# A graph layer and an attention layer on one core: two sets of transposes on TensorE, or through DRAM with block transposes on VectorE

## The chip, the cores and the metric

The kernel runs on one core of a Trainium2 chip. The metric is the device time of one execution in microseconds (us), lower is better. Three executions of the kernel before took 2546.09, 2548.84 and 2551.68 us; the median is 2548.84. The profile is that of another execution, with a span of 2546.3 us from the first to the last instruction. The engines are TensorE (PE in the profile, with its weight loads as PEld), VectorE (DVE), ScalarE (ACT), GpSimd (POOL) and SyncE (SP), which issues all DMAs of this kernel from one queue, in order.

## The reference

The input x is (16 batches, 1024 nodes, 256 channels), all in float32. Layer 0 is a graph convolution with two batch norms, a residual and a layer norm. Layer 1 weights the adjacency matrix by a function of the means of the rows, derives queries from it, and attends with 4 heads of 64 channels:

```python
x = _layernorm(x + _L0_gnn_ref(...))            # x1 below: the normalised rows
# layer 1, per batch; fea is x1 transposed
c_adj = mean over channels of x1
A = abs(abs(sigmoid(c_adj[m] - c_adj[n]) - 0.5) - 0.5) * 2.0
g = relu(einsum('cn,nm->cm', fea, adj * A) * para)   # queries, as g transposed
k, v = x1 @ kv_w, split
out = softmax(q k^T * scale) v                       # 4 heads
x = _layernorm(x1 + out)
```

Two transpositions follow from this. Keys and values are products of x1 with channels on the partitions (x1T), while the layer norm and the graph product need x1 with nodes on the partitions. And the sums of values (ot, channels on the partitions, nodes along the row) have to be turned back into rows of nodes before they are divided by the softmax denominators, added to x1 and normalised.

## The kernel before, in words

Layer 0 takes the first 815 us or so and is not touched. Its result y lies in DRAM (yT), with channels first. Layer 1 is `fast()`. It works through the 16 batches in a pipeline of three depths: while batch b attends, the graph product, keys and values of batch b+1 and the normalised rows of batch b+2 are made.

The order of the work is written out by hand. A batch has 16 *steps*; a step is 16 matmuls of scores (L739), two exponentials on ScalarE (L751), 16 matmuls of values (L770, into the PSUM tiles o) and two additions of the exponentials on VectorE into acc (L760, or L757 for the first step of a head pair). Half `hf` of the nodes and pair `pair` of the heads change every four steps: (half 0, pair 0), (0, 1), (1, 0), (1, 1). All other work is cut into pieces, which `put(w, t, f, ...)` places into *slots*, eight to a batch (slot 8w + t). Two slots and then four steps are issued in turn, so that a batch consists of four such groups. I call them quarters 0 to 3: quarter 0 is slots 0 and 1 and the steps of (half 0, pair 0), and so on. `arrange` orders the pieces of a slot: `dens` and `bn2_q` first, the pieces of TensorE (keys, values, graph) with the short ones (`short`) spread among them, the rest by `rank` (the list `order`), and the gates (`wg_a`, `wg_b`, ScalarE and VectorE) spread over the whole. The first addition of a quarter, `sums(g)`, is placed after the last short piece of its two slots. Every engine executes its share in the order of issue.

The pieces that matter here:

- `load` (slots 0 to 3, tiles j = 0 to 3 of 256 rows): four DMAs of 32x32 blocks of y from DRAM into the buffer yt (L432; the pool has two buffers) and one of x (L436).
- `bn2_q` (slot j+1): two operations on GpSimd over yt (L599).
- `rows` (slot j+2): VectorE's 32x32 block transpose from yt into x1 (L603) and the residual (L604). With the blocks fetched in the right places, this makes a full transposition. So y already takes this way.
- `ln1_a`, `ln1_b` (slots j+2, j+3): layer norm of x1; `means` (slot 6) and `crow` (slot 7): the row of means, transposed on TensorE (L659) and spread over all partitions by way of DRAM.
- `x1_t` (slot j+4): four transposes of 128x128 on TensorE into PSUM (px, L638), and a copy into x1T on ScalarE (L639; on VectorE for batch 0).
- `keys` and `values` (slots 0 to 2), `wg_a`/`wg_b` (slots 0 to 3), `graph` (slots 3 to 7) of batch b+1.
- At the end of a pair's four steps, `attend` joins both PSUM tiles of values into ot (a copy on ScalarE, L781, and an addition on VectorE, L782).
- `dens` (slots 4 and, for half 1, 8, that is slot 0 of the next batch): matmuls of acc with ones (pd, L791). They need all additions of the half just ended. `recips` (one slot later): transposes (pr) and reciprocals into RD (L804).
- `finish_a` (slots 5, 6 and 9, 10): four transposes of ot on TensorE (pf, L813), VectorE's multiplication by RD out of PSUM (L817), GpSimd's addition of x1 (L822). `finish_s`: statistics (L547, L548) and the factors on GpSimd. `finish_b`: normalisation on ScalarE (L838) and the store of the result (L841).

Before the first batch attends, the pieces of batch 1's rows are issued in eight slots of their own, beside the graph product of batch 0 (`opening`), without steps between them.

Of the kernel before, what the change touches and what calls it, by code (L numbers as in the profile page):

```python
# [9 lines left out]
F32 = mybir.dt.float32  # L10
# [6 lines left out]
P = 128  # L17
# [5 lines left out]
def gnn_norm_attention_kernel(  # L23
# [28 lines left out]
    dram = ctx.enter_context(tc.tile_pool(name="dram", bufs=1, space=DRAM))  # L52
    ctx.enter_context(tc.manual_schedule())

    ident = const.tile([P, P], F32, name="ident")
# [25 lines left out]
    Q = 32  # L81
    NQ = P // Q
    y_blk = [yT_all[b].rearrange("i (d e) (q n) -> q e (i d) n", e=Q, q=NQ) for b in range(B)]
    st2_dram = dram.tile([2, C], F32, name="st2_d")

    c_dram = [dram.tile([NT, P], F32, name=f"crow_d{b}") for b in range(B)]
# [33 lines left out]
    with ExitStack() as l0:  # L120
# [32 lines left out]
        with ExitStack() as ph1:  # L153
# [9 lines left out]
            for i in range(0, NT, 2):  # L163
                t = hp.tile([P, 2, N], F32, tag="h", name=f"A{i}")
# [22 lines left out]
            KB = FB // P  # L187
# [6 lines left out]
            for h in range(NH):  # L194
                rows = range(h * KB, (h + 1) * KB)
                for i in rows:
                    blk = A[i][:, ts(i, P)]
# [8 lines left out]
                for j in range(NT):  # L206
                    p = ps.tile([P, FB], F32, tag="ah"[j % 2], name="pat")
# [25 lines left out]
            for c in range(HT):  # L233
                p = ps.tile([P, FB], F32, tag="a", name="pw1")
# [3 lines left out]
            for c in range(CT):  # L238
                p = ps.tile([P, FB], F32, tag="a", name="pw2")
# [142 lines left out]
            for f in range(HT):  # L382
                for h in range(NH):
# [3 lines left out]
                    p = hidden(B - 1, h, f)  # L387
# [7 lines left out]
        ldp = right("ldp", LDP)  # L395
# [43 lines left out]
        with ExitStack() as ph2:  # L439
# [74 lines left out]
            for k, pair in enumerate(pairs):  # L514
# [23 lines left out]
    NP = HEADS // 2  # L538
# [17 lines left out]
    def fast():  # L556
      with ExitStack() as fx:
# [9 lines left out]
        otp = pool("otp", 3)  # L567
# [52 lines left out]
        def ln1_b(b, j):  # L620
            mv, rs = mvs.pop((b, j))
            for a in range(2):
# [8 lines left out]
                    accum_out=css[b][:, 2 * j + a : 2 * j + a + 1],  # L631
                )

        def x1_t(b, j):
            p = ps_t.tile([P, CT, 2 * P], F32, tag="t", name="px")
            for a in range(2):
                for c in range(CT):
                    nc.tensor.transpose(p[:, c, ts(a, P)], x1s[b, j][:, a, ts(c, P)], ident)  # L638
            (nc.vector.tensor_copy if b == 0 else nc.scalar.copy)(x1Ts[b][:, :, ts(j, 2 * P)], p)  # L639

        def means(b):
            nc.vector.tensor_scalar_mul(css[b], css[b], 1.0 / C)
# [84 lines left out]
        def step(g):  # L727
            b, s = divmod(g, NS)
            hf, pair, cp = s // (NP * NT // 2), s // (NT // 2) % NP, s % (NT // 2)
            return b, hf, pair, cp  # L730
# [22 lines left out]
        def sums(g):  # L753
# [4 lines left out]
            else:  # L758
                for a in range(2):
                    nc.vector.tensor_add(ACC[b, hf, pair], ACC[b, hf, pair], E[g, a])  # L760

        def attend(g):
            b, hf, pair, cp = step(g)
            if cp == 0:
                O[b, hf, pair] = [ps_t.tile([P, FB], F32, tag="t", name=f"o{g}_{r}") for r in range(2)]
            for a in range(2):
                cb = 2 * cp + a
                for r in range(2):
                    for h in range(2):
                        nc.tensor.matmul(  # L770
                            O[b, hf, pair][r][h * HD : (h + 1) * HD, :],
                            vs[b][r * HD : (r + 1) * HD, cb, pair * P + h * HD : pair * P + (h + 1) * HD],
                            E[g, a][r * HD : (r + 1) * HD, h, :],
                            start=(cb == 0),
                            stop=(cb == NT - 1),
                        )
                E.pop((g, a))
            if cp == NT // 2 - 1:
                t = otp.tile([P, FB], F32, tag=f"ot{pair}", bufs=2 - pair, name=f"ot{g}")
                o = O.pop((b, hf, pair))  # L780
                nc.scalar.copy(t, o[0])  # L781
                nc.vector.tensor_add(t, o[1], t)  # L782
                OT[b, hf, pair] = t

        def dens(b, hf):
            p = ps_t.tile([P, FB], F32, tag="t", name="pd")
# [10 lines left out]
        KB = FB // P  # L797

        def recips(b, hf):
# [5 lines left out]
                RD[:, i : i + KB, :], p.rearrange("p k (h r) -> p k h r", r=32)[:, :, :, 0]  # L805
            )

        def finish_a(b, j):
            hf, k = divmod(2 * j, KB)
            p = ps_t.tile([P, 2, C], F32, tag="t", name="pf")  # L810
            for a in range(2):
                for pair in range(NP):
                    nc.tensor.transpose(p[:, a, ts(pair, P)], OT[b, hf, pair][:, ts(k + a, P)], ident)  # L813
            pool_r = (rp, "r") if b < B - 1 else (x1p, "x1")
            r = pool_r[0].tile([P, 2, C], F32, tag=pool_r[1], name=f"r_{b}_{j}")
            rd = RD[:, b * NT + 2 * j : b * NT + 2 * j + 2, :].rearrange("p a h -> p (a h)")
            nc.vector.tensor_mul(  # L817
                r.rearrange("p a (h d) -> p (a h) d", h=HEADS),
                p.rearrange("p a (h d) -> p (a h) d", h=HEADS),
                rd.unsqueeze(2).to_broadcast([P, 2 * HEADS, HD]),  # L820
            )
            (nc.gpsimd if b < B - 1 else nc.vector).tensor_add(r, r, x1s.pop((b, j)))  # L822
            R[b, j] = r
# [52 lines left out]
        def put(w, t, f, *a):  # L876
            at.setdefault(w * NC + t, []).append((f, a))
# [4 lines left out]
        for b in range(B):  # L882

            for hf in range(NH):
                t = (hf + 1) * (NC // NH)
                put(b, t, dens, b, hf)
                put(b, t + 1, recips, b, hf)
                for k in range(KB // 2):
                    put(b, t + 1 + k, finish_a, b, hf * (KB // 2) + k)
                    put(b, t + 1 + k, finish_s, b, hf * (KB // 2) + k)  # L890
                    late = NC - t - 2 - k if b == B - 1 and hf == 0 else 0
                    put(b, t + 2 + k + late, finish_b, b, hf * (KB // 2) + k)
            if b == 0:
                continue

            put(b - 2, 2, begin, b)
            for j in range(NT // 2):
                put(b - 2, j, load, b, j)
                put(b - 2, j + 1, bn2_q, b, j)
                put(b - 2, j + 2, rows, b, j)  # L900
                put(b - 2, j + 2, ln1_a, b, j)
                put(b - 2, j + 3, ln1_b, b, j)
                put(b - 2, j + 4, x1_t, b, j)
            put(b - 2, NC - 2, means, b)
            put(b - 2, NC - 1, crow, b)

            i = 0
            for t, n in enumerate(WG):
                for i in range(i, i + n):
                    put(b - 1, t, wg_a, b, i)  # L910
                    put(b - 1, t, wg_b, b, i)
                i += 1
            kv = [(keys, (b, c, h)) for c in range(CT) for h in range(NH)]
            kv += [(values, (b, j)) for j in range(0, NT, 2)]
            for t, n in enumerate(KV):
                for _ in range(n):
                    f, a = kv.pop(0)
# [9 lines left out]
        nsteps = B * NS  # L927


        order = (dens, recips, finish_a, finish_b, x1_t, rows, ln1_a, ln1_b, finish_s, means, load, crow)  # L930
        rank = {f: k for k, f in enumerate(order)}
        short = (dens, recips, finish_a, x1_t, crow)
        long = (keys, values, graph)

        def spread(few, many):
# [143 lines left out]
        )  # L1079

    flag = fast()


# [153 lines left out]
```

## Time and profile before

| engine | busy us of 2546.3 | share |
|---|---|---|
| TensorE (PE) | 2487.9 | 98% |
| VectorE (DVE) | 1730.6 | 68% |
| ScalarE (ACT) | 1078.3 | 42% |
| GpSimd (POOL) | 865.3 | 34% |

| group of instructions | count | busy us | mean ns |
|---|---|---|---|
| TensorE transposes of x1, px L638 | 256 | 40.7 | 282 |
| TensorE transposes of ot, pf L813 | 256 | 40.2 | 280 |
| VectorE block transposes of y, L603 | 60 | 42.1 | 702 |
| VectorE additions into acc, L760 | 384 | 515.8 | 1343 |
| ScalarE copies into x1T, L639 | 60 | 35.1 | 586 |
| DMAs of 64 KB of y blocks, L432 | 240 | | |

Matmuls are pipelined, so that the busy time of a group on TensorE counts overlapping instructions; the distance between their starts is what one occupies. In the timeline, a row joins equal instructions that follow each other ("x4"), and a bracket at its end says how long the engine was idle before it and what ended the idle time. The DMA share of the 16 DMA engines is about 0.16 in the attention part, at 38 GB/s. A batch takes 105.8 us there, from one pd to the same pd of the next batch.

### The profile page before, as it was taken

How to read it: one execution, taken by the hardware profiler on the slowest of the kernel's cores; microseconds unless marked ns; L12 is line 12 of the kernel's file. 1: busy time of each engine (PE TensorE's matmuls, PEld its weight loads, DVE VectorE, ACT ScalarE, POOL GpSimd, SP SyncE). 2: the span in 40 equal slices, each digit the busy share in tenths (PEclk: the TensorE clock that was granted, in tenths of full speed). 3: DMA queues.
4: the chain of work that ended last, by engine and by line, in shares of the span. 5: the costliest groups of instructions: out<-in, count | busy, mean ns of one | idle time of the engine just before them, and what ended most of it. 6: DMA issues, size and time to landing. Idle time of an engine off the chain costs nothing. (4 is left out here: it accounts for less than half of the span.)

```text
span 2546.3 us, 33280 instructions
## 1 busy us (share of the span) xinstructions
PE 2487.9 (98%) x12813; PEld 1067.4 (42%) x12813; DVE 1730.6 (68%) x2594; ACT 1078.3 (42%) x1385; POOL 865.3 (34%) x766
## 2 busy tenths in 40 slices
PE   8999999998998999999999999999999999999997
PEld 4444444443443444344443444434444344443432
DVE  5545554556776776786877768777687776877556
ACT  2000000004453455465554655546556465564644
POOL 2222322222555323342433324333243332432132
PEclk9999999999999999999999999999999999999998
DMA  3122222230885201111111111111111111110000
GB/s 132 66 89 93 99 74 91 83 141 21 301 297 173 59 18 46 43 29 34 26 46 46 26 34 26 46 46 26 34 26 46 47 25 34 27 48 27 9 13 23
DMA packets 233349, 163.79 MB, mean 64 GB/s; under 512 B 136680, under 2 KB 221280, under 8 KB 226016
## 3 DMA queue, kind: packets, MB, share of 16 engines
q1 hardware_dynamic: 233184, 161.60, 21.1%
q8 instruction: 103, 1.69, 0.3%
q14 instruction: 62, 0.51, 0.1%
HBM read 98.58 MB, written 62.98 MB: 63 GB/s over the span
## 5 line engine op out<-in xcount | busy, mean ns | idle before, releaser
L751 ACT ACTIVATE e<-s 128x1024 f32<-128x1024 f32 x512 | 495.8, 1020 | 361.9 <-PE s L739 311.5
L760 DVE TENSOR_TENSOR acc<-acc,e 128x1024 f32<-128x1024 f32 x384 | 515.8, 1343 | 72.7 <-ACT e L751 42.6
L739 PE MATMUL s<-qT,kT 64*64 64x512 f32 x4096 | 492.4, 596 | 13.9 <-ACT e L751 13.2
L770 PE MATMUL o<-e,v 64*64 64x512 f32 x4096 | 486.4, 590 | 0.0
L713 PE MATMUL pg<-wg,x 128*128 128x512 f32 x960 | 434.5, 594 | 0.0
L822 POOL TENSOR_TENSOR r<-r,x 128x512 f32<-128x512 f32 x60 | 105.7, 1761 | 572.3 <-ACT wg L671 261.1
L739 PEld LDWEIGHTS s<-qT,kT 64*64 64x64 f32 x4096 | 147.2, 133 | 309.6 <-issue 250.9
L770 PEld LDWEIGHTS o<-e,v 64*64 64x64 f32 x4096 | 157.0, 133 | 284.1 <-issue 271.4
L599 POOL TENSOR_TENSOR yt<-yt,stq 128x512 f32<-128x512 f32 x120 | 192.4, 1603 | 193.2 <-DMA yt<-yT 188.3
L713 PEld LDWEIGHTS pg<-wg,x 128*128 128x128 f32 x960 | 172.3, 190 | 175.9 <-issue 166.1
L98 ACT COPY u<-pa 128x512 f32<-128x512 f32 x15 | 8.8, 585 | 475.3 <-PE pa L303 475.3
L680 DVE SCALAR_TENSOR_TENSOR wg<-wg,adj_sb 128x1024 f32<-128x1024 f32 x128 | 156.3, 1239 | 67.3 <-ACT wg L676 65.0
L303 PE MATMUL pa<-AhT,x 128*128 128x512 f32 x360 | 161.8, 592 | 0.0
L688 PE MATMUL pk<-x1T,kvw 128*128 128x512 f32 x256 | 118.4, 606 | 1.3 <-DVE x1T L639 1.3
L639 ACT COPY x1T<-px 128x512 f32<-128x512 f32 x60 | 35.1, 586 | 191.4 <-PE px L638 190.6
L699 PE MATMUL pv<-kvw,x1T 128*128 128x256 f32 x512 | 115.7, 379 | 0.0
L721 DVE TENSOR_TENSOR qT<-pg,para_sb 128x512 f32<-128x512 f32 x64 | 44.2, 690 | 101.7 <-PE pg L713 100.8
L334 PE MATMUL ph<-agg,SW 128*128 128x512 f32 x240 | 112.8, 592 | 0.0
L66 POOL TENSOR_SCALAR rs_a<-mv_a 128x2 f32<-128x2 f32 x64 | 20.5, 320 | 258.3 <-DVE mv_a L548 258.3
L303 PE MATMUL pa<-T,sx 128*128 128x512 f32 x240 | 107.9, 592 | 0.0
L303 PEld LDWEIGHTS pa<-AhT,x 128*128 128x128 f32 x360 | 68.4, 190 | 86.1 <-issue 86.1
L782 DVE TENSOR_TENSOR ot<-o,ot 128x512 f32<-128x512 f32 x64 | 44.0, 688 | 87.8 <-ACT ot L781 87.8
(193 smaller groups left out, 3332.4 us busy)
## 6 DMA issues: line engine op xcount, KB each, us to landing
h<-hT SPq DMA_DIRECT2D x28, 1024.0 KB, 4.4
hL<-h SPq DMA_DIRECT2D x28, 1024.0 KB, 9.2
x<-in_x_dram SPq DMA_DIRECT2D x16, 1024.0 KB, 7.3
yT<-y SPq DMA_DIRECT2D x64, 256.0 KB, 2.5
out_dram<-r SPq DMA_DIRECT2D x64, 256.0 KB, 2.1
xr<-in_x_dram SPq DMA_DIRECT2D x62, 256.0 KB, 2.9
yt<-yT SPq DMA_DIRECT2D x240, 64.0 KB, 2.9
crow<-crow_d SPq DMA_DIRECT2D x15, 512.0 KB, 4.0
```

Of the source, the lines that this page charges most:

```text
L303: nc.tensor.matmul(p, xs[n][:, k, :], bs[n][:, k, :], start=(k == 0), stop=(k == KN - 1))
L334: nc.tensor.matmul(p, ws[n][:, ts(f, P)], bs[n], start=True, stop=True)
L599: nc.gpsimd.tensor_tensor(y, y, sc, op)
L680: nc.vector.scalar_tensor_tensor(t, t, 1.0, adj_sb[:, i, :], op0=OP.add, op1=OP.mult)
L688: nc.tensor.matmul(p, kvw[:, k, ts(c, P)], x1Ts[b][:, k, ts(h, FB)], start=(k == 0), stop=(k == CT - 1))
L699: nc.tensor.matmul(p[:, ts(a, C)], x1Ts[b][:, k, ts(j + a, P)], kvw[:, k, C:], start=(k == 0), stop=(k == CT - 1),)
L713: nc.tensor.matmul(pg[b], x1s[b, k // 2][:, k % 2, ts(c, P)], wgs[b, k][:, ts(h, FB)], start=(k == 0), stop=(k == NT - 1))
L739: nc.tensor.matmul(t[r * HD : (r + 1) * HD, h, :], kTs[b, pair][h * HD : (h + 1) * HD, ts(2 * cb + r, HD)], qTs[b, pair, hf][h * HD : (h + ...
L751: nc.scalar.activation(E[g, a], S.pop((g, a)), AF.Exp)
L760: nc.vector.tensor_add(ACC[b, hf, pair], ACC[b, hf, pair], E[g, a])
L770: nc.tensor.matmul(O[b, hf, pair][r][h * HD : (h + 1) * HD, :], vs[b][r * HD : (r + 1) * HD, cb, pair * P + h * HD : pair * P + (h + 1) * HD],
L822: (nc.gpsimd if b < B - 1 else nc.vector).tensor_add(r, r, x1s.pop((b, j)))
```

## The change

Both transpositions leave TensorE. The normalised rows x1 of batches 1 to 15 are written to DRAM (`put_x1`, two DMAs per tile), read back by 32x32 blocks (`get_x1`, four DMAs, into a buffer of the pool that y uses) and turned by a block transpose on VectorE straight into x1T (`x1_v`). ScalarE's copy goes. The sums of values ot are written to DRAM at the end of a pair (one DMA in `attend`), read back by blocks (`fetch_o`, four DMAs, one buffer) and turned on VectorE inside `finish_a`, whose multiplication then reads SBUF. Only the last half of the last batch (`by_pe`) and the rows of batch 0 keep TensorE. Keys are made half by half instead of channel block by channel block. In the list of short pieces, `x1_t` is gone and nothing takes its place.

```diff
+        def put_x1(b, j):
+            for c in range(CT):
+                nc.sync.dma_start(
+                    x1_dram[b, j][c].rearrange("(a p) f -> p a f", p=P), x1s[b, j][:, :, ts(c, P)]
+                )
+
+        def get_x1(b, j):
+            t = XB[b, j] = ldp.tile([P, CT * 2 * P], F32, tag="yt", name=f"xb{b}_{j}")
+            blk = x1_dram[b, j].rearrange("c (m n) (q f) -> q n (c m) f", n=Q, q=NQ)
+            for q in range(NQ):
+                nc.sync.dma_start(
+                    t[q * Q : (q + 1) * Q].rearrange("p (m f) -> p m f", f=Q), blk[q]
+                )
+
+        def x1_v(b, j):
+            nc.vector.transpose(x1Ts[b][:, :, ts(j, 2 * P)], XB.pop((b, j)).rearrange("p (c n) -> p c n", c=CT))
...
-            (nc.vector.tensor_copy if b == 0 else nc.scalar.copy)(x1Ts[b][:, :, ts(j, 2 * P)], p)
+            nc.vector.tensor_copy(x1Ts[b][:, :, ts(j, 2 * P)], p)
...
+        def by_pe(b, hf):
+            return b == B - 1 and hf == NH - 1
...
-                t = otp.tile([P, FB], F32, tag=f"ot{pair}", bufs=2 - pair, name=f"ot{g}")
+                t = otp.tile([P, FB], F32, tag=f"ot{pair}", bufs=1, name=f"ot{g}")
...
-                OT[b, hf, pair] = t
+                if by_pe(b, hf):
+                    OT[b, hf, pair] = t
+                else:
+                    nc.sync.dma_start(
+                        o_dram[b, hf][:, ts(pair, P), :].rearrange("i p n -> p i n"),
+                        t.rearrange("p (i n) -> p i n", n=P),
+                    )
...
+        def fetch_o(b, j):
+            hf, k = divmod(2 * j, KB)
+            if by_pe(b, hf):
+                return
+            t = OB[b, j] = otp.tile([P, 2, C], F32, tag="ob", bufs=1, name=f"ob{b}_{j}")
+            blk = o_dram[b, hf].rearrange("i (d e) (q n) -> q e (i d) n", e=Q, q=NQ)
+            for q in range(NQ):
+                nc.sync.dma_start(
+                    t[q * Q : (q + 1) * Q].rearrange("p a (d n) -> p (a d) n", n=Q),
+                    blk[q][:, ts(k // 2, 2 * C // Q), :],
+                )
...
+                p = r
+                nc.vector.transpose(
+                    r.rearrange("p a c -> p (a c)"), OB.pop((b, j)).rearrange("p a c -> p (a c)")
+                )
...
+                    put(b, t + k, fetch_o, b, hf * (KB // 2) + k)
                     put(b, t + 1 + k, finish_a, b, hf * (KB // 2) + k)
...
-                put(b - 2, j + 4, x1_t, b, j)
+                put(b - 2, j + 3, put_x1, b, j)
+                put(b - 2, j + 4, get_x1, b, j)
+                put(b - 2, j + 5, x1_v, b, j)
...
-            kv = [(keys, (b, c, h)) for c in range(CT) for h in range(NH)]
+            kv = [(keys, (b, c, h)) for h in range(NH) for c in range(CT)]
...
-        order = (dens, recips, finish_a, finish_b, x1_t, rows, ln1_a, ln1_b, finish_s, means, load, crow)
+        order = (dens, recips, finish_a, fetch_o, finish_b, x1_v, rows, ln1_a, ln1_b, put_x1, get_x1, finish_s, means, load, crow)
         rank = {f: k for k, f in enumerate(order)}
-        short = (dens, recips, finish_a, x1_t, crow)
+        short = (dens, recips, finish_a, crow)
```

More of the change, by code (lines that the diff above doesn't have):

```diff
@@ L83, in gnn_norm_attention_kernel @@
     y_blk = [yT_all[b].rearrange("i (d e) (q n) -> q e (i d) n", e=Q, q=NQ) for b in range(B)]
+    o_dram = {(b, h): dram.tile([NT // NH, C, P], F32, name=f"o{b}_{h}") for b in range(B) for h in range(NH)}
+    x1_dram = {
+        (b, j): dram.tile([CT, 2 * P, P], F32, name=f"x1_{b}_{j}") for b in range(1, B) for j in range(NT // 2)
+    }
     st2_dram = dram.tile([2, C], F32, name="st2_d")
@@ L632, in ln1_b @@
                 )
+        XB = {}
+        def put_x1(b, j):
[12 more added lines that the diff above has]
+            nc.vector.transpose(x1Ts[b][:, :, ts(j, 2 * P)], XB.pop((b, j)).rearrange("p (c n) -> p c n", c=CT))
         def x1_t(b, j):
@@ L806, in recips @@
             )
+        OB = {}
+        def fetch_o(b, j):
[9 more added lines that the diff above has]
+                )
         def finish_a(b, j):
             hf, k = divmod(2 * j, KB)
[L810 to L813, printed above, removed]
             pool_r = (rp, "r") if b < B - 1 else (x1p, "x1")
             r = pool_r[0].tile([P, 2, C], F32, tag=pool_r[1], name=f"r_{b}_{j}")
+            if by_pe(b, hf):
+                p = ps_t.tile([P, 2, C], F32, tag="t", name="pf")
+                for a in range(2):
+                    for pair in range(NP):
+                        nc.tensor.transpose(p[:, a, ts(pair, P)], OT[b, hf, pair][:, ts(k + a, P)], ident)
+            else:
+                p = r
+                nc.vector.transpose(
+                    r.rearrange("p a c -> p (a c)"), OB.pop((b, j)).rearrange("p a c -> p (a c)")
+                )
             rd = RD[:, b * NT + 2 * j : b * NT + 2 * j + 2, :].rearrange("p a h -> p (a h)")
```

## The prediction

> **What bounds the kernel now.** I read the page's busy shares first, then TensorE's waits in the attention part, the timeline of one batch (number 6 of 0 to 15, 1511 to 1618 us) engine by engine, and the DMA issues.
>
> ```profile
> PE 2487.9 (98%) x12813; PEld 1067.4 (42%) x12813; DVE 1730.6 (68%) x2594; ACT 1078.3 (42%) x1385; POOL 865.3 (34%) x766
> ...
> PE s L739 <- ACT e L751: 5.6, 14, 0.6
> PE pd L791 <- DVE acc L760: 0.4, 2, 0.2
> ...
> 1559.87 1.90 PE L770 MATMUL o<-e,v 64*64 64x512 f32 x16
> 1561.70 1.05 PE L791 MATMUL pd<-acc,ones 128*32 128x512 f32 x4
> 1562.96 1.05 PE L791 MATMUL pd<-acc,ones 128*32 128x512 f32 x4 [0.21 <-DVE acc L760]
> 1563.95 0.66 PE L638 MATMUL px<-ident,x 128*128 128x128 f32 x4
> ```
>
> TensorE hardly waits: from batch to batch the same instruction returns every 105.8 us. But one of its two short waits matters: at the start of quarter 2 the sums matrix (pd) waits for VectorE's last addition. VectorE, 68% busy on average, is on the path there:
>
> ```profile
> 1521.18 1.23 DVE L680 SCALAR_TENSOR_TENSOR wg<-wg,adj_sb 128x1024 f32<-128x1024 f32 x1 [1.12 <-ACT wg L676]
> 1522.33 0.68 DVE L817 TENSOR_TENSOR r<-pf,RD 128x512 f32<-128x512 f32 x1
> 1522.93 1.22 DVE L757 TENSOR_TENSOR acc<-e,e 128x1024 f32<-128x1024 f32 x1
> 1525.32 0.43 DVE L547 BATCH_NORM_STATS2 st_z<-r 128x6 f32<-128x256 f32 x1 [1.17 <-POOL r L822]
> ...
> 1540.83 0.70 DVE L603 STREAM_TRANSPOSE x<-yt 128x512 f32<-128x512 f32 x1
> ...
> 1553.53 9.38 DVE L760 TENSOR_TENSOR acc<-acc,e 128x1024 f32<-128x1024 f32 x6
> 1562.83 0.69 DVE L782 TENSOR_TENSOR ot<-o,ot 128x512 f32<-128x512 f32 x1
> ```
>
> From 1525.3 to 1562.9 no idle time stands in front of any VectorE line: in quarters 0 and 1 it is full, and its end (1562.9) releases TensorE (1562.96). In quarters 2 and 3 it has some 18 us of idle in 54.
>
> ```profile
> 1497.08 2.02 SPq L432 DMA_DIRECT2D yt<-yT  x4
> ...
> yT<-y SPq DMA_DIRECT2D x64, 256.0 KB, 2.5
> yt<-yT SPq DMA_DIRECT2D x240, 64.0 KB, 2.9
> ```
>
> SP issues in order, about 0.5 us for each DMA of 32-float pieces. The loads for quarter 0 leave at 1497, in quarter 3 before it.
>
> **What the Trainium skill says.** "TensorE: Matmul & The Clock Gate", Part 4, gives a TensorE transpose some 275 ns in a kernel and says a copy must follow. The trace shows that duration (273 ns), but four start within 0.44 us: 0.109 us is what one occupies. "VectorE: DVE Perf Modes", The three transpose paths: VectorE transposes 32x32 blocks only; here 0.70 us for 128x512. "DMA: Bandwidth & Descriptors", Two DMAs through the same engine are not ordered: a read of what another DMA wrote must wait, on the issuing engine, for the first one's semaphore. The trace agrees: crow's read is issued 1.2 us after its write (1495.46, 1496.68). "SBUF — State Buffer", Who interferes with whom: a VectorE instruction with two SBUF inputs and a GpSimd one that reads SBUF shut each other out. The trace shows it: an addition L760 takes 1.23 us, beside L599 on POOL 1.88.
>
> **The change, part by part.** Against the profile's span, 2546.3 us; the three runs have a median of 2548.8, so I add the difference to that.
>
> (a) TensorE, quarters 2 and 3. Each batch from 0 to 13 loses here four x1 tiles (px) and two tiles of finish_a (pf): 24 transposes x 0.109 = 2.6 us. No wait of its own hides this: -2.6 x 14 = -36.6. The copies on ACT that go (0.59 us each) were beside other work: 0.
>
> (b) Quarters 0 and 1. Two pf tiles go (0.87 us), but TensorE only arrives earlier at the pd that waits for VectorE: worth 0. VectorE gains two transposes there; instructions overlap by 0.08, so 0.62 each. The x1 transpose that moves into quarter 0 falls in the idle time after 1512.9: 0. Multiplying from SBUF instead of PSUM is about the same (0.69), if POOL leaves the port. Against this, finish_s now comes after one gate pair more in the written order, so the 1.17 us wait for POOL is filled. In sum -1.17 + 0.62 + 0.62, and 0.5 for POOL's L599 now beside it (see c): 0.6 us later at pd. Batches 1 to 13: +7.8. Bounds: 0 (all filled) to 2.0 (two transposes, a blocked multiplication 0.66, nothing filled).
>
> (c) SP. Every batch gets 44 DMAs more: 8 puts and 16 gets of x1, 4 writes and 16 reads of o; at 0.48 us that is 21 us of a queue mostly idle. The order is what matters. The write of o waits for L782 (1512.95), lands 2.5 later; the four reads then go out 1515.5 to 1517.5 and land by about 1519.3 (L432's loads: 3.6 us from first issue to last landing); finish_a's transpose is due at 1522.4: 3 us of slack. The next batch's load, issued at 1497 before, stands behind them: landed at 1521.2. POOL's L599 for it (3.2 us) now runs ahead of finish_a's addition L822, which ends about 1526.7 rather than 1525.27; VectorE asks for it at about 1526.6 to 1527.2. So hidden, barely. In quarter 2 the reads land at 1571, due 1575; x1's come at 1574, due 1578. In quarter 3 the get for tile 2 lands at 1494.5 in the frame of the batch before, VectorE stands about 3 us for it, and its next work (L721) waited 5.1 us for TensorE anyway: 0.
>
> (d) crow's transpose moves to the front of slot 7, before its 14 matmuls of graph, since x1_t no longer shares them. It needs the means, which VectorE reaches after a transpose of o and one of x1: due at 1490.15, ready at 1490.2 to 1490.6. +0.3 x 14 = +4.2; bounds 0 and 1.0.
>
> (e) Batch 14 (its quarters have no x1 work, VectorE has slack): four pf tiles, -1.7.
>
> (f) The opening. There is no attention between the slots there. In before VectorE transposes at 866.67 and queries start at 872.87:
>
> ```profile
> 866.67 0.70 DVE L603 STREAM_TRANSPOSE x<-yt 128x512 f32<-128x512 f32 x1
> ...
> 872.87 0.69 DVE L721 TENSOR_TENSOR qT<-pg,para_sb 128x512 f32<-128x512 f32 x1 [0.87 <-PE pg L1006]
> ```
>
> Now x1_v of tile 0 stands before that transpose; its get goes out behind the put of tile 1 (ready at 866.7), so 866.8 + 0.9 + 3.6: 871.3. The same again for tile 1: put at 875.4, landed about 880. Queries then start at 882 and the first scores wait for them: +9, less if an order is kinder. Bounds -1.75 (the px saved, everything hidden) and 14.
>
> (g) The last batch: its quarters are short, so the way through DRAM shows. finish_a waits about 5 us longer in quarters 0 and 2, which delays a chain that stands still for 4.78 us today (TensorE at 2487.1 waits for ACT behind finish_b): 2.4, and 2.1 at the last pd. +4.5; bounds 0 and 8.
>
> Sum: -36.6 + 7.8 + 4.2 - 1.7 + 9 + 4.5 = -12.8. Predicted: 2548.8 - 12.8 = 2536.0 us.
>
> **Rivals.**
> - *All of it is collected.* (b) and (d) are 0, the ends cost 5: -36.6 - 1.7 + 5 = -33, 2516 us. For it: VectorE's average is 68%, and the 1.17 us is there to fill. Against: TensorE already waits at pd.
> - *VectorE takes the place of TensorE.* The multiplication is blocked by POOL and little is filled: (b) 1.5, (d) 0.6: -36.6 + 19.5 + 8.4 - 1.7 + 9 + 4.5 = +3, 2552 us. For it: no idle from 1525 to 1563. This is also the case in which the transposes are gone but the time isn't.
> - *Slower: SP's order starves POOL in quarter 0.* The load stands behind a write and its read-back; L599 behind the load; L822 behind L599; VectorE's st_z behind L822, and all sums behind that. Each us by which L822 ends after 1526.7 counts on 13 batches: from 1.0 us on nothing is won, from 1.4 on it is slower by over 0.2%. If the write and reads land 3 us later together, +39 gives 2575 us; with 2 us, 2562. For it: both L599 can take 2.0 us beside VectorE, and the write's landing (2.5) is only a median. Against: the queue is empty just then.
>
> **How the numbers follow.** Under 0.2% (5 us) a measurement of this kernel can't be told from no change. Forecast 0.42 (2525 to 2546), all collected 0.22, VectorE 0.18, SP 0.18. The first mostly and the second wholly are faster: with a little of the third 0.62. Same: a tenth of the first, over half of the third, a tenth of the fourth: 0.16. The rest is slower: 0.22. The range runs from the second case, 2512, to the milder half of the fourth, 2563; likeliest case alone 2525 to 2546.
>
> **What would show it.** px gone but for batch 0 and pf but for the last half. Between the pd of quarter 2 and the next pd some 2.3 us less than 55.8; from a quarter 0's pd to quarter 2's 0.6 more than 50.2, the wait of pd for L760 grown from 0.4 to about 1.4 us and quarter 0's wait for ACT's exponentials from 0.4 to 0.8. L599 of tile 0 in quarter 0 instead of quarter 3. No wait of the o transposes for a DMA outside the last batch. First scores near 884 instead of 875. It is wrong if L822 ends late in quarter 0 (the slower rival), if pd waits no longer (all collected), or if keys wait for x1's last tile, which I count at 0 since it is ready 1 us after they start and needed only by the second half.

## The result: slower, and the profile after

The changed kernel takes 2580.97 us (four runs, 2578.76 to 2583.27) against 2547.47 for the kernel before beside it: a ratio of 1.0129, 95% interval 1.0111 to 1.0146. The forecast was 2536.0, with a range to 2563. The profiled executions have spans of 2581.1 and 2546.3 us. Line numbers are now those of the changed kernel: the gate L680 is L705 (its first step L673 is L698), `bn2_q` L599 on GpSimd is L603 (the block transpose of y that was L603 is L607), finish_a's addition L822 is L878, scores L739 are L764, pd L791 is L827.

The engines' busy line of the page of the changed kernel, and then its waits of TensorE from 930 to 2400 us (total, times, longest):

```profile
PE 2454.4 (95%) x12325; PEld 1023.2 (40%) x12325; DVE 1817.4 (70%) x2716; ACT 1044.0 (40%) x1325; POOL 873.7 (34%) x766
```

```profile
PE pg L738 <- DVE wg L705: 35.5, 13, 3.3
PE s L764 <- ACT e L776: 10.6, 13, 0.8
PE pc L684 <- DVE cs L667: 8.8, 14, 0.9
```

TensorE did lose its work (2487.9 to 2454.4 us), but it now waits in 13 batches for a gate, 2.7 us on average. The same list of the kernel before has no such line, and the wait at pd that I had built on is gone from the list. The timeline of TensorE in batch 6 of the changed kernel, quarter 1 (start, duration, instruction, idle time before it):

```profile
1531.34 1.06 PE L827 MATMUL pd<-acc,ones 128*32 128x512 f32 x8
...
1561.85 4.45 PE L738 MATMUL pg<-wg,x 128*128 128x512 f32 x10
1568.99 1.12 PE L738 MATMUL pg<-wg,x 128*128 128x512 f32 x2 [2.69 <-DVE wg L705]
1570.05 3.60 PE L764 MATMUL s<-qT,kT 64*64 64x512 f32 x16
...
1585.60 1.06 PE L827 MATMUL pd<-acc,ones 128*32 128x512 f32 x8
```

Two losses stand here. The first is the 2.69 us in the middle of the graph product. The second has no bracket: the 16 scores after it take 3.60 us, where the same 16 take 1.90 to 2.00 elsewhere. VectorE in the same batch shows where the first comes from:

```profile
1540.98 2.10 DVE L705 SCALAR_TENSOR_TENSOR wg<-wg,adj_sb 128x1024 f32<-128x1024 f32 x1 [1.12 <-ACT wg L701]
1543.01 0.70 DVE L869 STREAM_TRANSPOSE r<-ob 128x512 f32<-128x512 f32 x1
...
1545.60 1.75 DVE L698 TENSOR_SCALAR wg<-wg 128x1024 int32<-128x1024 int32 x1
1547.39 1.23 DVE L705 SCALAR_TENSOR_TENSOR wg<-wg,adj_sb 128x1024 f32<-128x1024 f32 x1
...
1560.59 0.70 DVE L869 STREAM_TRANSPOSE r<-ob 128x512 f32<-128x512 f32 x1
...
1567.71 2.36 DVE L705 SCALAR_TENSOR_TENSOR wg<-wg,adj_sb 128x1024 f32<-128x1024 f32 x2
```

The pd of quarter 0 starts at 1531.34, before at 1511.54, so the two timelines are 19.80 apart. The first gate above starts just as before (1521.18 + 19.80), the pair at the end, before at 1545.47, is 2.44 us late. Step by step: the first gate takes 2.10 instead of 1.23, so the next instruction is 0.88 late; the first transpose adds 0.73, the multiplication 0.12; the exchange of finish_s with a gate pair gives 0.19 back; the long row of sums adds 0.15, the second transpose 0.74, and 0.01 comes from rounding. GpSimd (first a line of the kernel before, then two of the changed kernel) and SP's queue say why the first gate is slow:

```profile
1502.52 3.03 POOL L599 TENSOR_TENSOR yt<-yt,stq 128x512 f32<-128x512 f32 x2 [11.84 <-DMA yt<-yT]
```

```profile
1540.95 3.04 POOL L603 TENSOR_TENSOR yt<-yt,stq 128x512 f32<-128x512 f32 x2 [27.98 <-DMA yt<-yT]
1544.67 2.13 POOL L878 TENSOR_TENSOR r<-r,x 128x512 f32<-128x512 f32 x1 [0.68 <-ACT wg L700]
```

```profile
1532.78 0.38 SPq L816 DMA_DIRECT2D o<-ot  x1
1535.08 1.91 SPq L853 DMA_DIRECT2D ob<-o  x4
1537.04 2.08 SPq L436 DMA_DIRECT2D yt<-yT  x4
```

The load of tile 0 goes out behind o's write and read-back, at 1537.04, as the forecast said; before it left at 1497.08, which is 1516.9 in this frame. GpSimd starts on it at 1540.95, 0.03 us before the gate, which then takes 0.87 us longer. L878 at 1544.67 does the same to L698 (1.75 for 0.66). What the Trainium skill says in "SBUF — State Buffer", Who interferes with whom, of a VectorE instruction with two SBUF inputs fits the gate, which reads wg and adj_sb from SBUF while GpSimd reads two tiles there. L698 reads a single tile, and the trace shows it slow beside L878 as well.

The unbracketed loss is TensorE's clock. Stretches of 2 us from 1566 on, with TensorE's busy time first and the granted clock in the column before the DMA share:

```profile
1566.00:1568.00 2.00, 0.30 (x1) 0.00 (x0) 1.90 (x7) 0.00 (x0) 1.69 (x4) 1.00 0.74 169
1568.00:1570.00 2.00, 1.01 (x2) 0.30 (x2) 2.00 (x3) 0.00 (x0) 1.90 (x2) 1.00 0.07 22
1570.00:1572.00 2.00, 2.00 (x13) 0.74 (x16) 1.96 (x3) 1.76 (x3) 1.92 (x4) 0.50 0.03 8
1572.00:1574.00 2.00, 2.00 (x20) 0.54 (x16) 1.90 (x9) 1.55 (x3) 1.52 (x3) 0.64 0.38 131
1574.00:1576.00 2.00, 2.00 (x24) 0.62 (x20) 1.97 (x3) 0.75 (x1) 0.63 (x1) 1.00 0.49 131
```

From 1570 to about 1573.4 the clock is halved. The records of the granted clock count in stretches of 3.41 us; between 940 and 2400 us they add up to 34.1 us at half speed in the changed kernel, all in quarters 0 and 1 of 9 batches, and none before. Half of that, 17 us, is lost there.

The whole, from the starts of the pd matmuls in both traces (the terms are those of the forecast's sum; the unrounded pieces add up to the difference of the spans, 34.8):

| part | before | after | difference | forecast |
|---|---|---|---|---|
| to the first pd (opening, half a batch) | 928.0 | 943.1 | +15.1 | +9 |
| quarters 2 and 3, batches 0 to 13, mean | 55.59 | 53.14 | -34.3 | -36.6 + 4.2 |
| quarters 0 and 1, batches 1 to 13, mean | 50.16 | 53.85 | +47.9 | +7.8 |
| batch 14 | | | -1.5 | -1.7 |
| last batch, from its quarter 0 on | | | +7.6 | +4.5 |
| sum | | | +34.8 | -12.8 |

One piece of the second row comes from the quarter ahead of it. Where VectorE's sums are ready, all eight matmuls of pd start within 0.47 us. In the kernel before, the last four of the pd of quarter 2 start 1.06 to 1.26 us after the first in 13 of 14 batches, since VectorE's last addition ends only then, and what follows is about 1.05 us later for it. The waits of the matmuls hardly show this (0.21 us in the forecast's lines), because the first four still count as busy. The waits of TensorE's weight loads do (930 to 2400 us; before, then after):

```profile
PEld pd L791 <- DVE acc L760: 12.4, 13, 1.1
```

```profile
PEld pd L827 <- DVE acc L785: 3.7, 4, 0.9
```

In the changed kernel only four batches wait so, and they are those from 1 to 13 without a stretch at half clock: after such a stretch TensorE comes to pd when VectorE is done. So 9 x 1.05 = 9.5 of the 17 us come back in quarter 2.

### The profile page after: what moved, and what is told of

Same layout as the page of the kernel before. It is cut to its first block, busy times and chain, and to the rows that moved or that the text cites. A ratio compares the mean times of both kernels' runs of the same rounds, so it can differ in the third digit from the quotient of the medians.

```text
span 2581.1 us, 33464 instructions
## 1 busy us (share of the span) xinstructions
PE 2454.4 (95%) x12325; PEld 1023.2 (40%) x12325; DVE 1817.4 (70%) x2716; ACT 1044.0 (40%) x1325; POOL 873.7 (34%) x766
## 4 chain that ended last, share of the span: by engine, by line
PE 37%; DVE 23%; issue 7%; DMA 3%; ACT 2%; SPq 2%; POOL 1%; DVEq 0%; ACTq 0%; POOLq 0%
PE s L764 10%; PE o L800 9%; DVE acc L785 8%; PE pg L738 7%; PE po L483 7%; DVE wg L705 2%; PE pk L713 2%; DVE acc L782 2%; DVE st_z L551 2%; DVE x L628 1%; POOL r L878 1%; DMA o<-ot 1%; DVE wg L698 1%; DVE ot L812 1%; DVE r L869 1%
## 5 line engine op out<-in xcount | busy, mean ns | idle before, releaser
L785 DVE TENSOR_TENSOR acc<-acc,e 128x1024 f32<-128x1024 f32 x384 | 507.4, 1321 | 81.8 <-ACT e L776 52.0
L764 PE MATMUL s<-qT,kT 64*64 64x512 f32 x4096 | 505.4, 610 | 25.5 <-ACT e L776 23.9
L738 PE MATMUL pg<-wg,x 128*128 128x512 f32 x960 | 435.9, 603 | 35.5 <-DVE wg L705 35.5
L603 POOL TENSOR_TENSOR yt<-yt,stq 128x512 f32<-128x512 f32 x120 | 178.5, 1488 | 473.6 <-DMA yt<-yT 438.0
L764 PEld LDWEIGHTS s<-qT,kT 64*64 64x64 f32 x4096 | 149.0, 136 | 333.7 <-issue 271.0
L738 PEld LDWEIGHTS pg<-wg,x 128*128 128x128 f32 x960 | 177.6, 191 | 259.6 <-issue 212.6
L878 POOL TENSOR_TENSOR r<-r,x 128x512 f32<-128x512 f32 x60 | 116.7, 1945 | 339.9 <-issue 172.9
L705 DVE SCALAR_TENSOR_TENSOR wg<-wg,adj_sb 128x1024 f32<-128x1024 f32 x128 | 159.4, 1255 | 57.8 <-ACT wg L701 55.5
L894 ACT ACTIVATE r<-r,nm,rs_z 128x256 f32<-128x256 f32 x128 | 69.9, 594 | 190.5 <-POOL nm L886 190.4
L724 PEld LDWEIGHTS pv<-kvw,x1T 128*128 128x128 f32 x512 | 96.1, 190 | 32.9 <-issue 19.4
L483 PE MATMUL po<-hL,SV 128*128 128x512 f32 x224 | 98.4, 592 | 0.0
L68 POOL TENSOR_TENSOR rs_z<-rs_z,mhalf 128x2 f32<-128x2 f32 x64 | 92.4, 1443 | 5.3
```

The source lines that it names most:

```text
L483: nc.tensor.matmul(p, ws[n][:, k, :], bs[n][:, k, :], start=(k == 0), stop=(k == KF - 1))
L603: nc.gpsimd.tensor_tensor(y, y, sc, op)
L705: nc.vector.scalar_tensor_tensor(t, t, 1.0, adj_sb[:, i, :], op0=OP.add, op1=OP.mult)
L724: nc.tensor.matmul(p[:, ts(a, C)], x1Ts[b][:, k, ts(j + a, P)], kvw[:, k, C:], start=(k == 0), stop=(k == CT - 1),)
L738: nc.tensor.matmul(pg[b], x1s[b, k // 2][:, k % 2, ts(c, P)], wgs[b, k][:, ts(h, FB)], start=(k == 0), stop=(k == NT - 1))
L764: nc.tensor.matmul(t[r * HD : (r + 1) * HD, h, :], kTs[b, pair][h * HD : (h + 1) * HD, ts(2 * cb + r, HD)], qTs[b, pair, hf][h * HD : (h + ...
```

## The experiments

The first question is which of the two ways costs, and whether the opening is a loss of its own.

**x1 alone.** `by_pe` always true, so that o stays on TensorE:

```diff
-            return b == B - 1 and hf == NH - 1
+            return True
...
-                t = otp.tile([P, FB], F32, tag=f"ot{pair}", bufs=1, name=f"ot{g}")
+                t = otp.tile([P, FB], F32, tag=f"ot{pair}", bufs=2 - pair, name=f"ot{g}")
```

> Only the rows x1 go through DRAM; the sums of values are turned on TensorE again, with the two ot0 buffers of before. Theory A (the time is lost in quarters 0 and 1 of every batch, where the way of o adds VectorE work and moves GpSimd's work onto VectorE's gates; x1 costs something only in the opening): quarters 2 and 3 save 4 x 0.44 = 1.7 us less 0.3 to 0.6 for crow, so 14 x -1.2 = -17, opening +13: 2539 to 2547 us, and no wait of graph for a gate (L705). Theory B (x1's way is what costs: VectorE stands 52 us for its reads, crow waits for the means): 2560 us or more.

**o alone.** x1 of all batches on TensorE again:

```diff
-            nc.vector.tensor_copy(x1Ts[b][:, :, ts(j, 2 * P)], p)
+            (nc.vector.tensor_copy if b == 0 else nc.scalar.copy)(x1Ts[b][:, :, ts(j, 2 * P)], p)
...
+                if True:
+                    put(b - 2, j + 4, x1_t, b, j)
+                    continue
                 put(b - 2, j + 3, put_x1, b, j)
...
-        short = (dens, recips, finish_a, crow)
+        short = (dens, recips, finish_a, x1_t, crow)
```

> Only the sums of values go through DRAM; x1 is turned on TensorE for all batches and copied by ScalarE, as before. Theory A: quarters 0 and 1 keep their +3.7 us in the mean of 13 batches, quarters 2 and 3 lose 0.9, the end keeps +6, the opening is as before: 2547 + 36 + 6 = about 2589 us (2578 to 2595), with the wait of graph for a gate near 2.7 us a batch. Theory B: 2540 to 2552 us.

**TensorE in the opening.** The changed kernel, with the same edit for batch 1 alone (`if b == 1`).

> As the changed kernel, but the rows of batch 1 (the opening) are turned on TensorE. If the opening costs what the first pd shows (13.3 us later than before by the end of batch 0, most of it before the first scores): 2581 - 10 to 13 = 2568 to 2571 us, first scores back at about 875 us. If batch 0 had slack that takes the delay up anyway: within 3 us of 2581.

**Tile 0's load a slot earlier**, in slot 7 of the batch before, so that it is ahead of o's write in SP's queue:

```diff
-                put(b - 2, j, load, b, j)
+                put(b - 2, j - (j == 0 and b > 1), load, b, j)
```

> As the changed kernel, but the load of tile 0 of the next rows is issued one slot earlier, ahead of the write and read-back of o in SP's order. Theory A1 (the two L603 of this tile, which now run beside the gates of quarter 0, block one gate by 0.9 us): L603 of tile 0 moves back into quarter 3, the gate takes 1.23 us again, graph waits about 1.8 instead of 2.7 us, and in some batches the exponentials of quarter 1 no longer wait: -12 to -25 us, 2556 to 2569 us. Theory A2 (what delays VectorE is only its own two transposes and the addition L878): no more than 4 us, 2577 to 2581 us.

Measured, each with its ratio to the kernel before that ran beside it (95% interval; the row of before is that of the four new kernels' runs), the first pd, and the means of the quarters (2 and 3 of batches 0 to 13, 0 and 1 of batches 1 to 13):

| kernel | us | ratio | first pd | quarters 2, 3 | quarters 0, 1 | half clock, 940 to 2400 |
|---|---|---|---|---|---|---|
| before | 2548.6 | 1 | 928.0 | 55.59 | 50.16 | 0 |
| after | 2581.0 | 1.0129 (1.0111 to 1.0146) | 943.1 | 53.14 | 53.85 | 34.1 |
| x1 alone | 2536.0 | 0.9950 (0.9934 to 0.9967) | 941.1 | 53.85 | 50.13 | 0 |
| o alone | 2579.5 | 1.0118 (1.0101 to 1.0134) | 929.4 | 54.17 | 53.69 | 27.3 |
| TensorE in the opening | 2567.6 | 1.0079 (1.0059 to 1.0100) | 930.4 | 53.20 | 53.62 | 27.3 |
| load earlier | 2567.6 | 1.0075 (1.0058 to 1.0091) | 944.3 | 53.74 | 51.80 | 3.4 |

All four come out on the side of their first theory; x1 alone is 3 us below its range, as the wait for crow that theory A put in isn't there. x1's way gains even with its lossy opening; o's way loses. x1's saving in quarters 2 and 3 is 1.74 us, which is 16 transposes x 0.109. The opening is a cost by itself, 13.4 us. The earlier load takes another 13.4: the steady part's quarters 0 and 1 fall by 2.05, of which 1.18 is clock ((34.1 - 3.4) / 2 / 13) and 0.87 the gate that no longer meets GpSimd. VectorE (only its gate lines) and TensorE's waits in that kernel:

```profile
1534.64 1.23 DVE L705 SCALAR_TENSOR_TENSOR wg<-wg,adj_sb 128x1024 f32<-128x1024 f32 x1 [1.12 <-ACT wg L701]
1538.27 1.76 DVE L698 TENSOR_SCALAR wg<-wg 128x1024 int32<-128x1024 int32 x1
```

```profile
PE pg L738 <- DVE wg L705: 22.8, 13, 2.1
```

The gate is back at 1.23, L698 still meets L878, and the wait is 1.7 us rather than 2.7. Part of the gain, 0.60 us a batch, went back to quarters 2 and 3: with hardly a stretch at half clock left, pd waits for VectorE's sums in 12 batches again, not in 4, and (12 - 4) x 1.05 = 8.4 is 14 x 0.60:

```profile
PEld pd L827 <- DVE acc L785: 11.6, 12, 1.4
```

x1 alone also settles the exchange of finish_s with a gate pair. Its code still has the empty `fetch_o` pieces, so it has the exchange without o's transposes. VectorE in its batch 6:

```profile
1525.68 1.21 DVE L782 TENSOR_TENSOR acc<-e,e 128x1024 f32<-128x1024 f32 x1
1526.81 1.78 DVE L698 TENSOR_SCALAR wg<-wg 128x1024 int32<-128x1024 int32 x1
1528.62 1.23 DVE L705 SCALAR_TENSOR_TENSOR wg<-wg,adj_sb 128x1024 f32<-128x1024 f32 x1
1529.76 0.42 DVE L551 BATCH_NORM_STATS2 st_z<-r 128x6 f32<-128x256 f32 x1
```

The 1.17 us in front of st_z are filled, and L698 takes 1.78 for 0.66 because it now runs beside L878. Quarters 0 and 1 stay at 50.13: the wait turned into a blocked instruction.

**VectorE's work without the transfers.** On the kernel with o alone, the transpose reads the ot tile in place:

```diff
-            t = OB[b, j] = otp.tile([P, 2, C], F32, tag="ob", bufs=1, name=f"ob{b}_{j}")
...
+            OB[b, j] = OT[b, hf, k // 2]
```

The write in `attend` goes too, and ot0 has its second buffer again. In the kernel with o alone, ScalarE's copy into ot had waited for TensorE's values only, not for a buffer.

> x1 by TensorE as before; finish_a's transpose on VectorE reads the ot tile itself, and o is neither written to DRAM nor read back: the blocks stay in the wrong places (this leaves out the exchange of blocks), the VectorE work is that of the change. o's way with its transfers was 2579.5. Theory A (half of o's loss is VectorE's two transposes in quarters 0 and 1, half is SP's order, which brings tile 0's load behind o's transfers and POOL's work on it onto a gate): quarters 0 and 1 at 51.4 to 51.7, 2554 to 2564. Rival B (only the order of the transfers costs): quarters 0 and 1 at 50.2, 2536 to 2546. Rival C (only VectorE's work costs): 2572 or more.

2555.80 us (2552.91 to 2561.38), ratio 1.0021 (1.0013 to 1.0030); quarters 0 and 1 at 51.63 in nearly all batches, 54.69 in 2 and 3. Theory A. Two transposes cost 1.46 us a batch there without any transfer, the same as in the kernel with the earlier load (51.62). Its wait for the gate:

```profile
PE pg L738 <- DVE wg L705: 22.3, 13, 1.7
```

**ACT's last pass later.** I had first put the 3.60 us of scores down to exponentials queued behind finish_b. `finish_b` one slot later:

```diff
-                    put(b, t + 2 + k + late, finish_b, b, hf * (KB // 2) + k)
+                    put(b, t + 3 + k + late, finish_b, b, hf * (KB // 2) + k)
```

> The changed kernel with finish_b (ACT's last pass over a tile) one slot later. Theory A: the second stall of quarters 0 and 1 (1.65 us in about 8 of 13 batches, exponentials queued on ACT behind finish_b, which waits for POOL's nm) goes: 8 x 1.65 = 13 us under 2581, so 2564 to 2572. Rival B: the wait for POOL is not what makes them late, or finish_b meets other work in its new place: 2577 to 2586.

2577.10 us (2574.80 to 2580.43): rival B. Quarters 0 and 1 are no shorter (54.18 against 53.85). The gain of 4 us comes from the last batch, which is 9.4 us shorter in the profile. This sent me to the clock records, where the 3.60 us are plain.

**The transposes twice over**, to see whether the wait alone halves the clock:

```diff
-                nc.vector.transpose(
-                    r.rearrange("p a c -> p (a c)"), OB.pop((b, j))
-                )
+                for _ in range(1 + hf):
+                    nc.vector.transpose(r.rearrange("p a c -> p (a c)"), OB[b, j])
+                OB.pop((b, j))
```

> As o_local (blocks left in the wrong places), with each of the two transposes of half 1, which VectorE does in quarters 0 and 1, done twice over: 2 x 0.62 = 1.24 us more VectorE work ahead of the fifth gate, and no transfer or POOL work with it. o_local gave 2555.8, with one TensorE wait for that gate of 1.7 us a batch, and one halved clock window in the steady part. Theory A (TensorE's clock is set for stretches of 3.41 us and halved for the next one where TensorE idled for more than about 1.75 us of one): the wait grows to 2.9 us, and in most batches it is followed by a halved stretch that costs 1.7 us more: 13 x 1.24 + 9 to 12 x 1.7 = 31 to 37, so 2585 to 2595, quarters 0 and 1 at 52.9 in some batches and 54.6 in most. Rival B (the halved stretches of the changed kernel come from its transfers or POOL's work, not from the wait): 13 x 1.24 = 16, so 2568 to 2576, and all batches at 52.9.

2581.02 us (2579.96 to 2583.37), so 25 us more for 2 x 13 x 0.74 = 19 us of VectorE work. The total is below the range of theory A, as quarters 2 and 3 became 0.6 us shorter, which I had not foreseen: pd waits for the sums in 4 batches here, not in 12, and gives 8 x 1.05 us back. What the run was for came out as in A: 9 of 13 batches have 54.6 to 54.8 in quarters 0 and 1, the other four 53.1, with 30.7 us at half clock. TensorE in one of the nine, and its wait over all:

```profile
1564.47 2.08 PE L738 MATMUL pg<-wg,x 128*128 128x512 f32 x2 [3.20 <-DVE wg L705]
1566.48 2.63 PE L764 MATMUL s<-qT,kT 64*64 64x512 f32 x16
```

```profile
PE pg L738 <- DVE wg L705: 41.6, 13, 3.2
```

The added work is VectorE's alone, with no transfer and nothing for GpSimd. I then counted TensorE's idle time in every 3.41 us stretch of full clock, 945 to 2400 us, in all 14 kernels of this study. After more than 5800 stretches with under 1.7 us idle, none was halved. After all 39 with over 2.0 us idle, the next one was halved. Of 30 in between, 6 were. (Four stretches that were themselves halved stayed so for one more.) So a wait of 2.7 us usually costs another 1.7 in its quarter, of which the next pd here gives 1.05 back, and a wait of 1.7 us rarely costs more than itself.

**x1 alone, TensorE in the opening.** Both edits together.

> All of o by TensorE as before, x1 through DRAM from batch 2 on, batch 1's x1 in the opening by TensorE as before. Theory A (the costs add: the opening's 13 to 14 us are the way of batch 1's x1 and nothing else; the steady gain is x1's shorter quarters 2 and 3): x1 alone gave 2536.0, less 13 to 14: 2521 to 2525, with the first pd at 928 to 931, quarters 2 and 3 at 53.85 and quarters 0 and 1 at 50.13. Rival B (the opening's wait is given back later, as batch 1's head start is lost in its first quarters): 2531 to 2537.

2525.44 us (2520.30 to 2526.68), ratio 0.9902 (0.9885 to 0.9918): the two add, 0.4 us above theory A's upper end.

**o of half 0 only.** Half 0 is finished in quarters 2 and 3, where VectorE has slack:

```diff
-            return True
+            return hf == NH - 1 or b == B - 1
...
-                    put(b, t + 1 + k, finish_a, b, hf * (KB // 2) + k)
+                    put(b, t + 1 + k * (1 - hf), finish_a, b, hf * (KB // 2) + k)
```

> x1 as in the run beside it (DRAM from batch 2 on); o of half 0 (finished in quarters 2 and 3, where VectorE has slack) through DRAM, o of half 1 (finished in quarters 0 and 1, where the gates have none) by TensorE, with the last of its two finish_a one slot earlier so that one ot buffer a pair is enough. Theory A: quarters 0 and 1 stay at 50.1 to 50.3 and quarters 2 and 3 fall by a further 0.7 to 53.1, so 14 x 0.7 = 10 under x1 alone with TensorE's opening: 2510 to 2517. Rival B: o's transfers and transposes cost in quarters 2 and 3 as well, or the earlier finish_a waits for its buffers: 2522 or more.

2520.07 us (2517.64 to 2521.89): between the two. Quarters 0 and 1 stay at 50.13, as theory A has it, but 2 and 3 only reach 53.78. The one wait in the list of TensorE's matmuls in the steady part eats the difference:

```profile
PE pc L684 <- DVE cs L667: 8.5, 14, 0.6
```

This is crow's transpose at the front of slot 7, waiting for the means. Two ways to bring them forward. **x1's transpose behind the means**, in `order`:

```diff
-        order = (..., x1_t, x1_v, rows, ln1_a, ln1_b, put_x1, get_x1, finish_s, means, load, crow)
+        order = (..., x1_t, rows, ln1_a, ln1_b, put_x1, get_x1, finish_s, means, x1_v, load, crow)
```

> The kernel with o of half 0 alone through DRAM (2520.1), with x1's transpose on VectorE put behind the last tile's LN and the means in its step. There TensorE waited 0.60 us a batch for the means (crow's transpose), which took back what o's half saved in quarters 2 and 3 (53.78, with x1 alone 53.87). Theory A: the wait goes, quarters 2 and 3 fall to 53.0 to 53.3, 14 x 0.6 = 8 less: 2509 to 2515. Rival B (the later x1T holds up keys, or the means are late for another reason): 2518 to 2525.

2526.82 us (2523.51 to 2530.19): rival B, and slower than its range; the wait grew to 15.8 us in 14. In batch 6 VectorE finishes the means 0.47 us later. The edit also moves the transpose of the slot before: it had filled idle time of VectorE, and now delays that slot's sums by 0.7 us, as much as the other one frees. And without a transpose in between, the second step of the layer norm (L628) runs into L878 on GpSimd and takes 1.48 us; with the transpose there it was the first step, at 1.08. **The means ahead of finish_s**:

```diff
-        order = (..., x1_v, rows, ln1_a, ln1_b, put_x1, get_x1, finish_s, means, load, crow)
+        order = (..., x1_v, rows, ln1_a, ln1_b, put_x1, get_x1, means, finish_s, load, crow)
```

> The kernel with o of half 0 alone through DRAM (2520.1), now with the means ahead of finish_s's statistics in their step on VectorE (0.94 us), x1's transpose left where it was. Theory A (crow's transpose waits 0.60 us a batch because four statistics stand ahead of the means): the wait goes, quarters 2 and 3 at 53.0 to 53.3, 2509 to 2515. Rival B (what VectorE does later, or POOL's work for finish_s, then comes in the way of something else): 2518 or more.

2511.82 us (2510.21 to 2512.62), ratio 0.9855 (0.9839 to 0.9872): theory A, and the fastest kernel of the study, 36 us under the kernel before. Quarters 2 and 3 are at 53.03, 0 and 1 at 50.13, and in the steady part the list of TensorE's waits comes down to one line. Its weight loads still wait at pd and at the gate once a batch:

```profile
PE pd L827 <- DVE acc L785: 0.2, 1, 0.2
```

```profile
PEld pd L827 <- DVE acc L785: 12.1, 13, 1.2
...
PEld pg L738 <- DVE wg L705: 10.8, 13, 0.9
```

So some 13 x 1.05 = 14 us at pd stay in this kernel too; no run tried to take them.

**The whole change with three placings altered**: the earlier load, TensorE in the opening, the means ahead of finish_s.

> The whole change, both values and rows on VectorE, with three of its placings altered: tile 0's load a slot earlier (alone 13.4 us less), batch 1's x1 by TensorE (alone 13.4 less), the means ahead of finish_s's statistics (0.6 us of wait for crow in 14 batches, 8 less). Theory A (three separate costs, they add): 2581 - 35 = 2546, so 2541 to 2551, quarters 0 and 1 at 51.6 and quarters 2 and 3 at 53.1: no gain over the kernel before, since the two transposes of half 1 still hold up the fifth gate by 1.5 us. Rival B (they are one cost seen in three places): 2555 or more.

2536.89 us (2535.90 to 2538.52), ratio 0.9957 (0.9940 to 0.9974). Both quarters are where theory A put them (53.06 and 51.62); the total is 4 us below its range, and the first pd comes at 926.0, 4.4 us earlier than with TensorE in the opening alone. 1.9 us of that lie ahead of the first scores (873.7 against 875.6), and 1.7 are half clock (3.4 us there, none here). So the change could gain 11 us as a whole, and 25 us more if half 1 of o stays on TensorE.

## Why the prediction was wrong

**The step that failed is (b), quarters 0 and 1: +7.8 forecast, +47.9 measured.** Three of its terms were wrong. The runs' texts call the gate in question the fifth; it is gate 5 counted from 0, the sixth of eight, the first of the pair that VectorE makes in quarter 1.

- *The place.* I let VectorE's delay count at pd alone, where the trace of before showed a wait. This gate is another point where the engines meet, with no slack either. In the kernel before, the eleventh of the twelve matmuls of the graph product in quarter 1, the first that needs it, starts 0.05 to 0.06 us after the gate's end in each of 13 batches. That is the distance at which it starts in the changed kernel after its wait. TensorE loses only 0.01 us by it, so the matmuls' list of waits has no line; the list of the weight loads has one for each batch (batch 6 of before, then its weight loads from 930 to 2400 us):

```profile
1542.45 5.43 PE L713 MATMUL pg<-wg,x 128*128 128x512 f32 x12
```

```profile
1545.47 2.36 DVE L680 SCALAR_TENSOR_TENSOR wg<-wg,adj_sb 128x1024 f32<-128x1024 f32 x2
```

```profile
PEld pg L713 <- DVE wg L680: 8.8, 13, 0.7
```

By letting TensorE arrive 0.87 us earlier without pf, the change could only make the wait there longer.

- *The size.* -1.17 for the filled wait and +0.5 for port contention should have been about -0.2 and +0.9: filling the wait put L698 beside L878 (1.75 for 0.66), and GpSimd's L603 met a gate (2.10 for 1.23). A transpose cost 0.73 to 0.74, not 0.62; the trace of before has it, where L604 starts at 1541.57, 0.74 after the transpose at 1540.83. Together VectorE was 2.44 us late, not 0.6. My upper bound, 2.0, left out the gate.
- *The clock.* I took a microsecond of wait to cost a microsecond. 17 of the 48 us are TensorE at half speed after the wait, and 9.5 of these came back at pd, in the row of quarters 2 and 3. The Trainium skill, "TensorE: Matmul & The Clock Gate", Part 1, puts the fall to half clock after an idle window of about 3.4 us. Here over 2.0 us idle in a stretch of 3.41 was enough each time, so the measurement decides.

The 47.9 add up as: gate 35.5, half clock 17.1, longer waits for exponentials 5.0 (10.6 for 5.6), less the eight transposes of pf, 13 x 0.87 = 11.3: 46.3. The remaining 1.6 I have not traced.

**(a) and (d), quarters 2 and 3, held as a sum, in part by luck**: -34.3 against -32.4. The transposes were worth 0.109 us each (x1 alone: -1.74 for 16; o in place: -0.90 for 8). (d) was 0.63 a batch, 8.8 in all, not 0.3. Against that, pd's wait fell away in 9 batches, -9.5, where the forecast had it grow to 1.4 us; that came from the half clock and not from the transposes. -36.6 + 8.8 - 9.5 is -37.3; the other 3.0 I have not traced.

**(c), SP's queue, was right in the order and its times, and wrong in "hidden".** Tile 0's load went out at 1537.04, 1517.2 in the forecast's frame (forecast 1517.5). GpSimd worked on it in quarter 0, and L878 ended at 1527.0 in that frame (forecast 1526.7). The o transposes waited for DMAs only 9.1 us in the whole run, in the last batch. I asked only whether L878 would end in time for st_z. Nothing waited for that; what GpSimd's L603 hit was a gate. The slower rival named this queue and this work, at a chance of 0.18, but its mechanism (st_z behind L878) isn't what cost: VectorE has no idle time in front of st_z.

**(f), the opening, was 9 and is 15.1.** The first scores come at 883.84, as forecast. TensorE waits for the means before them:

```profile
882.07 0.37 PE L684 MATMUL pc<-ident,cs 128*8 128x128 f32 x1 [9.92 <-DVE cs L667]
883.84 3.88 PE L764 MATMUL s<-qT,kT 64*64 64x512 f32 x16 [1.40 <-DVE qT L746]
```

What I had not counted is the second line's 3.88 for 16 scores: of the 17 us at half clock there, about 10 lie after the first scores and lose 5 of the 6.3 us that are left. **(e)** held. **(g)** was 3 us too low: the waits for ACT's exponentials doubled (4.8 to 9.4), and pd waited 3.0.

## What to carry to other kernels

Before moving work onto an engine that is full for a stretch, follow its timeline to every point where another engine takes something from it, those with no wait and no slack too; the waits of the matmuls name only the points that already hurt, those of TensorE's weight loads name the others too. Filling a wait is worth nothing if what fills it then runs beside the work that was waited for and is shut out by it. And move the work only where the receiving engine has idle time: with half of o and the opening left on TensorE and the means brought forward, this change gained 36 us; all of it moved, it lost 33.5.

## What the runs showed of the hardware

Two waits of TensorE that look alike are not: 1.7 us a batch was followed by half clock in at most one batch of 13 (three kernels, 0 to 3.4 us), 2.7 to 3.2 us in 8 or 9 of 13 (five kernels, 27 to 41 us). The clock is set for stretches of 3.41 us, and where in them a wait falls decides, so that quarters 0 and 1 of equal batches of one run differ by 1.65 us (52.59 and 54.24). A matmul held up by another engine need not show idle time in front of it: pd's last four started 0.6 to 0.8 us later than they could (1.06 to 1.26 us after the first, for 0.45) behind a bracket of at most 0.21, and the wait stood with the weight loads (12.4 us in 13 batches). And work of GpSimd beside VectorE's can more than double the time of an instruction: an int32 operation with a single tile as its input went from 0.66 to 1.75 us beside a GpSimd addition.
